# Edge-pair network on one core: a bias product moved from TensorE to GpSimd and VectorE for three of five chunks

## The chip, the cores and the metric

One core of a Trainium2 chip runs the whole program. The metric is the device time of one execution in microseconds. Runs that are compared are "fast" ones unless the text says otherwise; a run counts as slow when it takes over 1.5% longer than the fastest run of the same kernel. A ratio below is the mean time of one kernel's fast runs over the mean of the other kernel's fast runs of the same rounds, so it is not quite the ratio of the medians quoted beside it.

## The reference, cut to what matters

128 graphs of 64 nodes with 128 features. Every pair of nodes goes through a three-layer network with two layer norms, the result is weighted by the adjacency matrix and summed per node, and a second network of the same form updates the node.

```python
def _mlp(x, w0, b0, g0, be0, w1, b1, g1, be1, w2, b2):
    h = relu(x @ w0 + b0);  h = layernorm(h, g0, be0)
    h = relu(h @ w1 + b1);  h = layernorm(h, g1, be1)
    return h @ w2 + b2
messages = _mlp(concat(f_i, f_j), msg...) * adj[..., None]      # 64 x 64 pairs per graph
agg = sum(messages, axis=2)
updated = x + _mlp(concat(x, agg), upd...)
```

## The kernel before

Only real edges are computed, gathered into tiles of 128 edges: five tiles a graph, 20 for a "quartet" of four graphs, handled in chunks of four tiles, so five chunks a quartet. The first layer norm's scale is not applied to h. Instead the next bias is multiplied with each edge's standard deviation (std0), so that the scale can be taken out later: z = h·W1 + std0·b1. In the kernel before, TensorE makes std0·b1 too. The deviations are split into a high and a low part, transposed, and used as the stationary operand of one matmul of 512 columns in front of each chunk's layer-1 matmuls:

```python
def root_of(q):
    sd = root0(stp, V0[q], QT, "m20")                       # ScalarE: sqrt
    SH[q] = lp.tile([P, 4, QT], F32R, name="sh", bufs=2)
    sdb = sd.unsqueeze(1).to_broadcast([P, 2, QT])
    nc.scalar.copy(SH[q][:, 0:2, :], sdb)                   # high part
    nc.gpsimd.tensor_tensor(SH[q][:, 2:4, :], sdb, SH[q][:, 0:2, :].bitcast(F32),
                            op=ALU.subtract)                # low part
def turn_root(q):
    SD[q] = abank()
    nc.tensor.transpose(SD[q][0:4 * QT, 0:P], SH.pop(q)..., ident)
def layer1(n):
    q, c = divmod(n, QC)
    ps = ps_z.tile([P, CH, C], F32, name="z")               # one buffer
    nc.tensor.matmul(ps, lhsT=SD[q], rhs=W["b1t"][:, CH*c:CH*c+CH, :], start=True, stop=False, ...)
    for t in range(CH):
        nc.tensor.matmul(ps[:, t, :], lhsT=h[:, t*P:(t+1)*P], rhs=W["w1c"], start=False, ...)
    nc.scalar.activation(Y[n], ps, AF.Relu)                 # ScalarE empties z
```

Every instruction's place is fixed by hand in a plan of steps, one chunk a step; a block of eight graphs is ten steps. Each engine is given its instructions in that order, and the trace of the kernel before shows GpSimd's rows in it (`place` from 305.67 us, `marks_table` from 307.32, `odd_marks` from 308.62, the next w at 312.72):

```python
at(o - 8, "e", place, b); at(o - 8, "e", marks_table, b); at(o - 8, "e", odd_marks, b)   # GpSimd
at(n, "e1", var0_of, q); at(n + 1, "b", root_of, q)
at(n + 1, "x", turn_root, q); at(n + 2, "a", root_out, q)
# ... (updates, weights and reductions are placed in the same way)
for n in range(last + 1):
    run(n, "a"); run(n, "m")
    layer1(n - L1); run(n, "b"); layer0(n); stats0(n - 1); marks(n + 2); compare(n + 2); stats1(n - L1)
    for k in ("x", "x1", "x2", "e1", "e"): run(n, k)
```

## Time and profile before

| | before |
|---|---|
| median, range | 644.69 us, 641.02 to 645.77 (four runs, timed beside the change) |
| TensorE busy, mean granted clock | 96%, 0.993 |
| VectorE, ScalarE, GpSimd busy | 78%, 56%, 58% |
| one block of ten steps | 37.20 us, the same from step 36 on |

The block length is read from the timeline of TensorE: the distance from one start of a once-per-block operation to the next. It is the most useful number, since nearly the whole span repeats it.

The page's rows of 40 equal slices show busy tenths and, for PEclk, the granted clock in tenths:

```profile
PE   7899999999999999999999999999999999998875
PEclk8999999999999999999999999999999999999998
```

TensorE is busy 96% of the span at a mean granted clock of 0.993.

### The profile page before, as it was taken

Reading aid. Unit: us, or ns where it says so; the run is one execution under the profiler, and the core shown is the slowest. Engines: PE = TensorE matmul, PEld = TensorE weight load, DVE = VectorE, ACT = ScalarE, POOL = GpSimd, SP = SyncE. Lnnn points to the kernel's source line nnn. Section 1 sums busy time; section 2 is a strip of 40 time slices with the busy share of each in tenths; the row PEclk is TensorE's granted clock in tenths of the full one; section 3 lists DMA queues with packets and bytes.
Section 4 is the critical chain, followed back from the end, with each engine's and each line's share of the span. In section 5 each row is a group of like instructions: output and inputs, shape, how many; then the busy total and the mean of one; then the engine's idle time right before and its main releaser. Section 6 shows DMA issues by size and latency. Waiting matters only on the chain.

```text
span 639.0 us, 15850 instructions
## 1 busy us (share of the span) xinstructions
PE 615.1 (96%) x5875; PEld 567.0 (89%) x5875; DVE 497.6 (78%) x1894; ACT 358.6 (56%) x811; POOL 368.4 (58%) x943
## 2 busy tenths in 40 slices
PE   7899999999999999999999999999999999998875
PEld 6688899999999999999999999999999999997764
DVE  6787687878878787887878788787878877785574
ACT  3556556655656565565656556565655656563532
POOL 6742463847657384765738476573837657363653
PEclk8999999999999999999999999999999999999998
DMA  5100000010010101001010100101010000000001
GB/s 119 40 21 6 2 10 2 2 43 3 2 42 2 42 3 42 2 7 37 2 43 2 43 3 11 32 2 44 2 34 1 17 4 2 17 1 18 2 18 35
DMA packets 27916, 12.06 MB, mean 19 GB/s; under 512 B 10422, under 2 KB 27836, under 8 KB 27836
## 3 DMA queue, kind: packets, MB, share of 16 engines
q1 hardware_dynamic: 27548, 10.89, 6.4%
q8 instruction: 47, 0.77, 0.5%
q14 instruction: 33, 0.27, 0.1%
q10 hardware_dynamic: 288, 0.13, 0.1%
HBM read 6.82 MB, written 4.19 MB: 17 GB/s over the span
## 4 chain that ended last, share of the span: by engine, by line

## 5 line engine op out<-in xcount | busy, mean ns | idle before, releaser
L526 DVE BATCH_NORM_STATS2 st<-hT 128x6 f32<-128x128 f32 x640 | 141.1, 282 | 65.2 <-PE hT L522 62.6
L562 PEld LDWEIGHTS z<-w1c,h 128*128 128x128 f32 x1280 | 168.4, 192 | 7.1
L562 PE MATMUL z<-w1c,h 128*128 128x128 f32 x1280 | 168.8, 275 | 0.0
L641 POOL TENSOR_TENSOR w<-oh,m_q 128x320 f32<-128x320 f16 x124 | 86.9, 722 | 127.4 <-PE hT L522 110.9
L572 DVE BATCH_NORM_STATS2 st<-y 128x6 f32<-128x128 f32 x640 | 137.6, 276 | 6.0 <-ACT y L565 6.0
L565 ACT ACTIVATE y<-z 128x512 f32<-128x512 f32 x160 | 95.6, 597 | 81.4 <-PE z L562 79.5
L516 ACT ACTIVATE h<-hps,b0c 128x512 f32<-128x512 f32 x160 | 109.2, 682 | 6.1 <-PE hps L513 6.0
L505 DVE TENSOR_TENSOR s<-mk,cmpt 128x512 fp32r<-128x512 f32 x160 | 107.4, 672 | 0.4 <-PE mk L498 0.4
L522 PE MATMUL hT<-ident,h 128*128 128x128 f32 x640 | 97.0, 274 | 0.0
L513 PE MATMUL hps<-s,abl 128*128 128x512 f32 (+3 forms) x256 | 91.7, 370 | 0.0
L522 PEld LDWEIGHTS hT<-ident,h 128*128 128x128 f32 x640 | 76.2, 141 | 9.7
L559 PE MATMUL z<-b1t,sdT 80*128 80x512 f32 x160 | 78.8, 493 | 0.9 <-ACT y L565 0.9
L513 PE MATMUL hps<-s,abh 128*128 128x512 f32 (+3 forms) x256 | 78.1, 323 | 0.0
L656 PE MATMUL ys<-y,w 128*64 128x128 f32 x1280 | 76.9, 275 | 0.0
L656 PEld LDWEIGHTS ys<-y,w 128*64 128x64 f32 x1280 | 69.2, 137 | 3.4
L498 PE MATMUL mk<-tp,qs 128*128 128x512 f16 (+3 forms) x256 | 61.2, 300 | 1.8 <-DVE s L505 1.7
L473 DVE TENSOR_TENSOR abl<-mu,abh 128x512 fp32r<-128x512 f32 x32 | 22.1, 690 | 49.6 <-ACT abh L466 49.5
L632 ACT CAST oh<-ma 128x384 f16<-128x384 f32 (+1 forms) x128 | 48.6, 433 | 4.7 <-PE ma L625 1.8
L513 PEld LDWEIGHTS hps<-s,abl 128*128 128x128 f32 x256 | 49.2, 192 | 0.6 <-ACT h L516 0.3
L466 ACT CAST abh<-mu 128x512 fp32r<-128x512 f32 x32 | 18.7, 585 | 54.8 <-PE mu L459 54.8
L513 PEld LDWEIGHTS hps<-s,abh 128*128 128x128 f32 x256 | 49.1, 192 | 0.0
L559 PEld LDWEIGHTS z<-b1t,sdT 80*128 80x128 f32 x160 | 30.3, 190 | 8.9 <-issue 3.1
(235 smaller groups left out, 1036.8 us busy)
## 6 DMA issues: line engine op xcount, KB each, us to landing
xn<-in_x_dram SPq DMA_DIRECT2D x15, 256.0 KB, 3.2
out_dram<-uo SPq DMA_DIRECT2D x15, 256.0 KB, 2.2
an<-in_adj_dram SPq DMA_DIRECT2D x16, 128.0 KB, 2.9
xn<-in_x_dram SPq DMA_DIRECT2D x2, 128.0 KB
out_dram<-uo SPq DMA_DIRECT2D x2, 128.0 KB, 2.1
w<-in_L_gnn_msg_w_dram SPq DMA_DIRECT2D x2, 64.0 KB, 2.9
u<-in_L_gnn_upd_w_dram SPq DMA_DIRECT2D x2, 64.0 KB, 2.0
w0a<-in_L_gnn_msg_w_dram ACTq DMA_DIRECT2D x1, 64.0 KB, 2.1
```

What stands on the lines that cost most here:

```text
L498: nc.tensor.matmul(MK[n][:, c:c + w], lhsT=blocks[g // (2 * PB)]["qs"][:, g // 2 % PB, g % 2, :], rhs=TP[g // 2][:, e:e + w], start=True, ...
L505: nc.vector.tensor_tensor(S[n], MK.pop(n), cmpt[:, o:o + CH * P], op=ALU.is_equal)
L513: nc.tensor.matmul(ps[:, c:c + w], lhsT=ab[:, g % 4, :], rhs=s[:, c:c + w], start=(k == 0), stop=(k == 1))
L516: nc.scalar.activation(H[n], ps, AF.Relu, bias=b0c)
L522: nc.tensor.transpose(ps[:, t, :], H[n][:, t * P:(t + 1) * P], ident)
L526: nc.vector.bn_stats(ST0[q][:, CH * c + t, :], ps[:, t, :])
L559: nc.tensor.matmul(ps, lhsT=SD[q], rhs=W["b1t"][:, CH * c:CH * c + CH, :], start=True, stop=False, skip_group_check=True)
L562: nc.tensor.matmul(ps[:, t, :], lhsT=h[:, t * P:(t + 1) * P], rhs=W["w1c"], start=False, stop=True, skip_group_check=True)
L565: nc.scalar.activation(Y[n], ps, AF.Relu)
L572: nc.vector.bn_stats(ST1[q][:, CH * c + t, :], Y[n][:, t, :])
L641: (nc.vector if p // 2 == NQ - 1 else nc.gpsimd).tensor_tensor(w[:, :, g, :], OH[p][:, :, g, :], Q[q][:, k:k + TG].unsqueeze(2).to_broadca ...
L656: nc.tensor.matmul(YS[b][g * N:(g + 1) * N, k, :], lhsT=w[:, t, g, :], rhs=y, start=(t == 0), stop=(t == TG - 1))
```

## The change

The intent: TensorE is the bound, so take 96 of its 160 bias matmuls away. In chunks 0, 2 and 4, GpSimd computes the product std0·b1 and VectorE adds it to z and applies the relu, in place of ScalarE's eviction. To pay for that on VectorE, the odd-weight flag is counted on GpSimd, and the update's output is scaled on ScalarE and added to the residual on GpSimd.

```diff
-        def odd_weights(b):                        # VectorE
-            nc.vector.tensor_reduce(nball[:, b:b + 1], blocks[b].pop("a2")..., op=ALU.max, ...)
+        def even_marks(b):                         # GpSimd
             nc.gpsimd.tensor_tensor(a2, an, an, op=ALU.mult)
             nc.gpsimd.tensor_tensor(a2, a2, an, op=ALU.subtract)
+            nc.gpsimd.tensor_scalar(a2, a2, 0.0, None, op0=ALU.is_equal)
+            nc.gpsimd.tensor_tensor(even, even, a2, op=ALU.add)
+        PB1 = (1, 3)
+        KT = len(PB1) * CH
+        K1 = 4 * KT                                # 32 rows instead of 80
         def root_of(q):                            # splits only the 8 tiles of chunks 1 and 3
+            for k, c in enumerate(PB1):
+                nc.scalar.copy(SH[q][:, 0:2, s], sd)
+                nc.gpsimd.tensor_tensor(SH[q][:, 2:4, s], sd, SH[q][:, 0:2, s].bitcast(F32), ...)
+        def shift1(n):
+            SDB[n] = sbp.tile([P, CH, C], F32, name="sdb")
+            nc.gpsimd.tensor_tensor(SDB[n], bc(W["b1b"], CH), SD[q][...].to_broadcast(...), op=ALU.mult)
         def layer1(n):
-            nc.tensor.matmul(ps, lhsT=SD[q], ...)
+            if c in PB1:
+                nc.tensor.matmul(ps, lhsT=SDT[q], rhs=W["b1t"][:, k:k + CH, :], ...)
             for t in range(CH):
                 nc.tensor.matmul(ps[:, t, :], ..., start=c not in PB1, ...)
-            nc.scalar.activation(Y[n], ps, AF.Relu)
+            if c in PB1:
+                nc.scalar.activation(Y[n], ps, AF.Relu)
+            else:
+                add_relu(Y[n], ps, SDB.pop(n))     # VectorE
+        def scale_out(u):                          # ScalarE, then an add on GpSimd in finish
+            nc.scalar.activation(u.o[:, q, :], u.l_ps[:, q, :], AF.Copy, scale=u.q1[:, q:q + 1])
+            for c in range(QC):
+                if c not in PB1:
+                    at(n + 1 + c, "e1", shift1, q * QC + c)
# ... (table of the bias, the flag's last reduction and the tail's VectorE branch are cut)
```

## The prediction

> **What bounds the kernel now.** I read the page's busy shares first, then the groups by line, the waits, and the timelines of TensorE and GpSimd over one period.
>
> The first fence is from the page: busy time by engine, then four groups (line, engine, operation, out<-in, count | busy us, mean ns | idle before).
>
> ```profile
> PE 615.1 (96%) x5875; PEld 567.0 (89%) x5875; DVE 497.6 (78%) x1894; ACT 358.6 (56%) x811; POOL 368.4 (58%) x943
> ...
> L641 POOL TENSOR_TENSOR w<-oh,m_q 128x320 f32<-128x320 f16 x124 | 86.9, 722 | 127.4 <-PE hT L522 110.9
> ...
> L565 ACT ACTIVATE y<-z 128x512 f32<-128x512 f32 x160 | 95.6, 597 | 81.4 <-PE z L562 79.5
> ...
> L505 DVE TENSOR_TENSOR s<-mk,cmpt 128x512 fp32r<-128x512 f32 x160 | 107.4, 672 | 0.4 <-PE mk L498 0.4
> ...
> L559 PE MATMUL z<-b1t,sdT 80*128 80x512 f32 x160 | 78.8, 493 | 0.9 <-ACT y L565 0.9
> ```
>
> TensorE is busy 96% of the span and waits for almost nothing, so it sets the time. GpSimd at 58% looks free, with 127 us of idle time before its weights products (w). The question is where that idle time lies.
>
> The schedule is fixed in program order. One step handles a chunk of four edge tiles; five steps are a quartet of graphs, ten steps a block, and the pattern repeats with the block. I count steps 0 to 9 so that the two large "reduce" steps are 3 and 8. The timeline of TensorE (start, us, engine, line, operation):
>
> ```profile
> 284.51 0.48 PE L559 MATMUL z<-b1t,sdT 80*128 80x512 f32 x1
> 284.83 1.05 PE L562 MATMUL z<-w1c,h 128*128 128x128 f32 x8
> ...
> 293.10 0.48 PE L559 MATMUL z<-b1t,sdT 80*128 80x512 f32 x1
> ...
> 299.17 0.27 PE L546 MATMUL ma<-ident,sh 128*80 128x128 f32 x1
> ...
> 317.88 0.27 PE L546 MATMUL ma<-ident,sh 128*80 128x128 f32 x1
> ```
>
> Step 8 starts at 284.51, step 0 at 293.10. The next step 8 starts at 321.71 in the same view, so a block takes 37.20 us, and 16 blocks 595 of the 639 us. The L546 rows at the ends of steps 1 and 6 transpose the square roots (sh), whose low parts GpSimd writes; TensorE stands behind them in order. The timeline of GpSimd, same block:
>
> ```profile
> 295.42 1.40 POOL L641 TENSOR_TENSOR w<-oh,m_q 128x320 f32<-128x320 f16 x2 [6.98 <-PE hT L522]
> ...
> 298.74 0.27 POOL L541 TENSOR_TENSOR sh<-m_sd,sh 128x40 fp32r<-128x40 f32 x1 [0.68 <-ACT sh L540]
> ...
> 309.30 0.72 POOL L418 TENSOR_TENSOR a<-a,an 128x256 f32<-128x256 f32 x1
> ...
> 311.70 0.23 POOL L272 TENSOR_TENSOR m_v<-m_v,m 128x20 f32<-128x20 f32 x1
> 312.72 1.40 POOL L641 TENSOR_TENSOR w<-oh,m_q 128x320 f32<-128x320 f16 x2 [0.80 <-DVE m_q L283]
> ...
> 316.30 0.27 POOL L541 TENSOR_TENSOR sh<-m_sd,sh 128x40 fp32r<-128x40 f32 x1 [0.68 <-ACT sh L540]
> ```
>
> This carries the prediction. GpSimd's idle time is one hole of 6.98 us in front of step 0's weights. From there to step 5's weights it works through 17 us with only 0.68 and 0.80 us idle: residual and bias of the update, placement, marks table, odd marks, variance. Its second sh ends at 316.57, only 1.31 us before TensorE's transpose at 317.88; in step 1 it ends at 299.01, 0.16 us before. The wait list agrees that this is every block: step 0's w waits 110.9 us in 17 times, step 5's 16.5 us in 14 (1.2 us each).
>
> [...] a 128x512 add takes GpSimd 1284 ns (xo), a two-input VectorE compare of that size 672. [...] The trace has 0.32 us from the bias matmul to the next (284.51 to 284.83), [...] I use 0.32. GpSimd's rows come in program order. [...]
>
> **The change part by part.**
> - TensorE: three of five bias matmuls go, six a block: 6 x 0.32 = 1.92 us of 37.20. Over 16 blocks 31 us, were nothing else to wait.
> - ScalarE: 96 evictions of 597 ns go. The update's output is scaled there instead, about 1.1 us a block (four times about 0.27 us, the 265 ns of a 128x128 PSUM copy). It has room.
> - VectorE: 96 add-and-relu of 128x512 come in, 0.67 us each as the existing uy one (64 us); 16 reduces of 0.40 us and 60 scalings of 0.34 us go (27 us). About 535 us, still under the span.
> - GpSimd, per block: six products of bias and std0 of 128x512, each 1.04 us as the same product in the update (usdb, 1039 ns); two further sh operations, 0.27 each; two more operations for the even count, an add of 0.73 and a comparison with a constant of 128x256, which has no row (about 0.8, my estimate from 260 ns at 20 columns and 618 at 128 with a per-partition scalar); an add of 1.28 in the output. In all 9.6 us on top of 23 us, so about 33 of 37. That fits on average, but not where it falls.
>
> The order of GpSimd's instructions in the changed kernel puts one product in step 0, ahead of the variance, one in step 1, one in step 3, and the even count in step 2: all inside the full stretch. One more is in step 5 before that variance. So:
> - Now from the w at 295.42 to the end of the second sh at 316.57: 21.15 us.
> - Added: 4 products 4.16, two sh 0.54, even count 1.55; the idle 0.80 is filled. 21.15 + 6.25 - 0.80 = 26.60 us.
> - TensorE wants that sh now 22.46 us after the w (317.88 - 295.42). It will wait until 26.60.
> - From that transpose to the next block's w is 37.20 - 22.46 = 14.74 us, set by TensorE and VectorE; two bias matmuls less (steps 7, 8) make 14.10.
> - New block: 26.60 + 14.10 = **40.70 us**, against 37.20: +3.5 us.
> Part of the wait shows in step 1: sh is 1.04 + 0.27 later, TensorE 0.32 earlier, slack 0.16, hence some 1.4 us idle there; the rest in steps 5 and 6. The product for step 5 comes after the same backlog, so VectorE's add waits for it, and with it the only z buffer. This overlaps the sh wait and isn't added.
>
> The full stretch needs both updates (from step 23) and placement (to about step 142): 12 blocks, +42 us. The four lighter ones keep little of the TensorE saving because step 1's wait stays; I take -2. Sum: +40 us, **684 us**.
>
> **The rivals.**
> - TensorE stays the bound: -31 us, 613. For it: 96% busy, and GpSimd's mean load under 90%. Against: the 0.16 and 1.31 us of slack before the two transposes. It needs the backlog to vanish.
> - VectorE becomes the bound: z has one buffer, and in three of five steps its release moves to VectorE, behind the update's layers. VectorE's 535 us lie under the span and TensorE's reduce steps of 6 us let it catch up; alone it would hold the time near 620 to 640. It would waste the gain, not lengthen the span much.
> - The clock: waits of 2 to 3 us in each block may drop TensorE's granted clock, now 0.993. [...]
>
> **Range and chances.** If the comparison costs 0.5 us more or less, the total moves 6 us; if a further 0.8 us of overlap is found per block, 10 us[...]. So 662 to 704. I leave 12% for a GpSimd stretch that starts earlier than I think: 0.05 faster, 0.07 within 2%.
>
> **What would show it.** Right: GpSimd runs without a gap from step 0 to step 5's weights, its hole before step 0 shrinks to about 4 us; TensorE waits for sh (L541's successor) or for VectorE's add, itself waiting for sdb, some 5 us a block; TensorE falls below 90% busy; a block takes 40 to 41 us. Wrong: sdb products well under 1 us, sh ready before TensorE arrives, TensorE still at 95%, blocks under 37 us. If blocks are near 37 us with VectorE waits naming z, the second rival holds.

The cut passages told of the hardware from elsewhere, or put a size on the fallen clock that no trace had given. The sum has lost no term: +42 - 2 = +40 us, 684 us. The range 662 to 704 has: beside the two terms that still stand (6 and 10 us) it held an estimate for the clock. That waits of 2 to 3 us can drop the clock was the author's guess then; the changed kernel's trace shows it (half clock at a wait of 2.95 us, below).

## The result, and the profile after

The changed kernel takes 742.19 us (741.97 to 743.59, four runs) against 644.69 us for the kernel before. The ratio of the fast runs is 1.153, 95% interval 1.148 to 1.158. The outputs agree with the reference. The direction was predicted; the size was not: +97.5 us where +40 was forecast.

A block now takes 44.37 us (44.37 to 44.42 from step 56 on). In the views below, sdb is GpSimd's product, z the PSUM buffer of layer 1 and y its output after the relu, sh the split roots, and w the weights product with which a block begins on GpSimd; CUSTOM_DVE_ANT_0 (in e2_noprod also _1) is the profile's name for what the kernel's `add_relu` issues at L247. First the page after: the busy line, the slices, and five groups.

```profile
PE 657.5 (89%) x5779; PEld 581.2 (78%) x5779; DVE 549.4 (74%) x1912; ACT 324.9 (44%) x809; POOL 509.7 (69%) x1116
...
PE   7799899898989989899898989989899898999774
...
PEclk9899999999998989989898998989989898999977
...
L653 POOL TENSOR_TENSOR w<-oh,m_q 128x320 f32<-128x320 f16 x124 | 87.0, 723 | 82.7 <-PE mk L495 75.9
...
L563 POOL TENSOR_TENSOR sdb<-b1b,m_sd 128x512 f32<-128x512 f32 x96 | 99.9, 1041 | 0.0
...
L247 DVE CUSTOM_DVE_ANT_0 y<-z,sdb 128x512 f32<-128x512 f32 x96 | 64.8, 675 | 14.5 <-PE z L578 4.9
...
L575 PE MATMUL z<-b1t,sdT 32*128 32x512 f32 x64 | 34.5, 540 | 38.9 <-DVE y L247 37.9
...
L581 ACT ACTIVATE y<-z 128x512 f32<-128x512 f32 x64 | 38.3, 598 | 67.7 <-PE z L578 67.7
```

No engine is above 89%. GpSimd's product costs 1041 ns as read off its sibling before (usdb, 1039 ns), and VectorE's add 675 ns. The new thing is the fourth group: TensorE stands idle for 38 us in front of bias matmuls until VectorE has emptied z. And the clock row has lost its even nines: the mean granted clock is 0.932.

Step 6 on TensorE in the kernel before (start, us, engine, line, operation):

```profile
313.17 0.48 PE L559 MATMUL z<-b1t,sdT 80*128 80x512 f32 x1
313.48 1.05 PE L562 MATMUL z<-w1c,h 128*128 128x128 f32 x8
```

One block on TensorE after, steps 5 to 9 (the same columns, then idle before and releaser):

```profile
309.28 0.60 PE L713 MATMUL ma<-ident,ysum 128*128 128x128 f32 x4
312.83 0.79 PE L575 MATMUL z<-b1t,sdT 32*128 32x512 f32 x1 [2.95 <-DVE y L247]
313.55 2.08 PE L578 MATMUL z<-w1c,h 128*128 128x128 f32 x8
...
320.64 0.27 PE L551 MATMUL ma<-ident,sh 128*32 128x128 f32 x1
...
330.00 0.49 PE L575 MATMUL z<-b1t,sdT 32*128 32x512 f32 x1
330.42 1.16 PE L578 MATMUL z<-w1c,h 128*128 128x128 f32 x8
```

In front of step 6 TensorE waits 2.95 us for VectorE's add. Then the same eight matmuls that took 1.05 us before take 2.08. The transpose of sh at 320.64 shows no wait at all.

VectorE's add of step 5, and GpSimd's timeline of the same block:

```profile
312.09 0.69 DVE L247 CUSTOM_DVE_ANT_0 y<-z,sdb 128x512 f32<-128x512 f32 x1 [0.38 <-POOL sdb L563]
```

```profile
290.70 1.40 POOL L653 TENSOR_TENSOR w<-oh,m_q 128x320 f32<-128x320 f16 x2 [5.09 <-PE mk L495]
...
310.83 0.23 POOL L272 TENSOR_TENSOR m_v<-m_v,m 128x20 f32<-128x20 f32 x1
311.01 1.04 POOL L563 TENSOR_TENSOR sdb<-b1b,m_sd 128x512 f32<-128x512 f32 x1
312.01 1.41 POOL L653 TENSOR_TENSOR w<-oh,m_q 128x320 f32<-128x320 f16 x2
...
316.77 0.36 POOL L546 TENSOR_TENSOR sh<-m_sd,sh 128x8 fp32r<-128x8 f32 x2 [0.86 <-ACT sh L545]
...
335.10 1.40 POOL L653 TENSOR_TENSOR w<-oh,m_q 128x320 f32<-128x320 f16 x2 [5.11 <-PE mk L495]
```

GpSimd works from the w at 290.70 to the one at 312.01, just behind the sdb that step 5 needs, with one idle time of 0.65 us (at 295.14, for ScalarE's part of sh), and then has a hole of 5.1 us in front of the next block. The sdb ends at 312.05, VectorE starts at 312.09, TensorE at 312.83. That is the whole chain of the wait.

The view of windows shows the clock of this block. The columns after the stretch are its length, then busy us of TensorE, its weight loads, VectorE, ScalarE and GpSimd, then the granted clock, the DMA share and GB/s.

```profile
305.00:310.00 5.00, 4.88 (x42) 4.28 (x41) 2.65 (x10) 2.26 (x6) 4.57 (x11) 1.00 0.00 0
310.00:315.00 5.00, 2.17 (x8) 1.73 (x8) 3.19 (x12) 1.85 (x4) 4.75 (x11) 0.72 0.00 0
315.00:317.50 2.50, 2.50 (x12) 2.34 (x12) 0.82 (x2) 1.72 (x5) 1.47 (x5) 0.50 0.00 0
317.50:320.00 2.50, 2.50 (x18) 2.34 (x16) 2.26 (x9) 0.00 (x0) 1.99 (x3) 0.70 0.00 0
320.00:325.00 5.00, 5.00 (x45) 4.82 (x44) 4.44 (x16) 2.38 (x8) 1.20 (x6) 1.00 0.02 3
```

TensorE was granted half its clock from about 312.2 to 319.0, 6.8 us. It got it back after the wait was long over. In the same place of ten blocks in the trace there is a stretch of 6.8 us at half clock, and in the two blocks before these one of 3.4 us.

The trace's record of the granted clock shows something more. It lists each drop with its start and length. In the changed kernel's trace there are 17, and the later 16 start a whole multiple of 3.413 us after the first (to 0.01 us), so the drops of this trace lie on a grid, and 44.37 us is 13 times 3.413. (The trace before has two drops, 182 times 3.413 us apart.) The blocks settled at 44.37 us (they took 43.1 us while the drop lasted 3.4 us). That the grid holds them there is my reading; no run tests it.

So the block as measured: 21.35 us from the w to the end of step 5's sdb, 0.78 through VectorE to TensorE's start, 7.81 for step 6 (312.83 to 320.64; it was 4.71 before, 313.17 to 317.88), 14.46 to the next w. The sum is 44.40.

### The profile page after: what moved, and what is told of

Same layout as the page of the kernel before. It is cut to its first block, busy times and chain, and to the rows that moved or that the text cites. A ratio compares the mean times of both kernels' runs of the same rounds, so it can differ in the third digit from the quotient of the medians.

```text
span 740.4 us, 15865 instructions
## 1 busy us (share of the span) xinstructions
PE 657.5 (89%) x5779; PEld 581.2 (78%) x5779; DVE 549.4 (74%) x1912; ACT 324.9 (44%) x809; POOL 509.7 (69%) x1116
## 4 chain that ended last, share of the span: by engine, by line
## 5 line engine op out<-in xcount | busy, mean ns | idle before, releaser
L578 PE MATMUL z<-w1c,h 128*128 128x128 f32 x1280 | 191.3, 295 | 5.4 <-DVE y L247 5.2
L519 PE MATMUL hT<-ident,h 128*128 128x128 f32 x640 | 102.3, 285 | 0.0
L563 POOL TENSOR_TENSOR sdb<-b1b,m_sd 128x512 f32<-128x512 f32 x96 | 99.9, 1041 | 0.0
L510 PE MATMUL hps<-s,abl 128*128 128x512 f32 (+3 forms) x256 | 96.5, 386 | 0.0
L519 PEld LDWEIGHTS hT<-ident,h 128*128 128x128 f32 x640 | 80.6, 147 | 10.3 <-DVE st L523 0.2
L510 PE MATMUL hps<-s,abh 128*128 128x512 f32 (+3 forms) x256 | 81.7, 337 | 0.0
L247 DVE CUSTOM_DVE_ANT_0 y<-z,sdb 128x512 f32<-128x512 f32 x96 | 64.8, 675 | 14.5 <-PE z L578 4.9
L575 PE MATMUL z<-b1t,sdT 32*128 32x512 f32 x64 | 34.5, 540 | 38.9 <-DVE y L247 37.9
L581 ACT ACTIVATE y<-z 128x512 f32<-128x512 f32 x64 | 38.3, 598 | 67.7 <-PE z L578 67.7
L575 PEld LDWEIGHTS z<-b1t,sdT 32*128 32x128 f32 x64 | 12.6, 197 | 51.9 <-DVE y L247 46.0
```

The lines of the kernel that those rows point to most:

```text
L247: nc.vector._custom_dve(TENSOR_ADD_SAT, out=o, in0=ps, in1=sb, s0=BIG, s1=0.0)
L510: nc.tensor.matmul(ps[:, c:c + w], lhsT=ab[:, g % 4, :], rhs=s[:, c:c + w], start=(k == 0), stop=(k == 1))
L519: nc.tensor.transpose(ps[:, t, :], H[n][:, t * P:(t + 1) * P], ident)
L563: nc.gpsimd.tensor_tensor(SDB[n], bc(W["b1b"], CH), SD[q][:, CH * c:CH * c + CH].unsqueeze(2).to_broadcast([P, CH, C]), op=ALU.mult)
L578: nc.tensor.matmul(ps[:, t, :], lhsT=h[:, t * P:(t + 1) * P], rhs=W["w1c"], start=c not in PB1, stop=True, skip_group_check=True)
```

## The experiments

Theory A: the program order of GpSimd's queue puts more work between step 0 and step 5 than fits; its late product makes VectorE's add late, and with it the only z buffer; the idle time so made drops TensorE's clock, which costs a second time. Rival B: VectorE's added 0.67 us in three of five steps is the bound in itself. All kernels below gave correct results except where said. The diffs are shortened to the lines that matter. "Before" was timed beside each group (medians 643.1 to 645.2 us).

| kernel | median us | ratio to before (95%) | block us | clock in the profile |
|---|---|---|---|---|
| the change | 742.19 | 1.153 (1.148 to 1.158) | 44.37 | 0.932 |
| e1_fill | 709.27 | 1.102 (1.098 to 1.107) | 41.49 | 0.991 |
| e2_noprod (wrong on purpose) | 673.32 | 1.045 (1.040 to 1.050) | 38.91 | 0.982 |
| e3_noeven | 683.28 | 1.062 (1.057 to 1.066) | 39.71 | 0.988 |
| e4_late | 738.53 | 1.143 (1.135 to 1.151) | 42.2 to 45.1 | 0.953 |
| e5_move | 673.65 | 1.048 (1.042 to 1.054) | 38.82 | 0.986 |
| e6_movelate | 684.42 | 1.063 (1.058 to 1.069) | 39.18 | 0.976 |
| e7_prods (on before) | 677.10 | 1.053 (1.047 to 1.059) | 39.55 | 0.988 |
| e8_noscale | 738.13 | 1.147 (1.142 to 1.152) | 44.37 | 0.939 |
| e9_before_move (on before) | 646.00 | 1.003 (0.998 to 1.009) | 37.20 | 0.986 |
| e10_k80 | 676.96 | 1.052 (1.047 to 1.058) | 38.4, or 40.0 where the clock falls | 0.967 |
| e11_best | 650.96 | 1.013 (1.008 to 1.017) | 36.88 | 0.986 |
| e12_best_nv | 640.32 | 0.995 (0.990 to 0.999) | 36.85 | 0.984 |

### e1_fill: keep TensorE busy in the gap

```diff
+        def keep_busy():
+            warm2 = ubank()
+            for k in range(10):
+                nc.tensor.matmul(warm2[:, 0:P], lhsT=mean_m, rhs=mean_m, start=True, stop=True)
+        for b in range(2, NB - 1):
+            at(b * CPB + 5, "x2", keep_busy)
```

> The changed kernel with ten idle 128x128 matmuls (about 2.1 us) put into step 5 of each block, in the gap where TensorE waits for VectorE's add. Theory A (GpSimd's queue makes a gap of 3 us; in the gap TensorE's granted clock falls to half for 6.8 us, which costs another 3.4 us a block): clock back to 0.98 or more, blocks fall from 44.4 to about 41 us (26.4 of GpSimd's stretch plus 14.5), time 698 to 712 us. Rival B (VectorE, with the added add-and-relu, sets the block and the low clock is only a sign of an idle TensorE): clock goes up, time stays within 1% of 742.

Adding work made it 33 us faster: 709.27 us. From the views of the cores, the changed kernel and this one:

```profile
core 0: 740.4 us, clock 0.932
```

```profile
core 0: 703.7 us, clock 0.991
```

The idle matmuls took 2.40 us a block. Blocks fell from 44.37 to 41.49 us; the views from 340 to 385 us show the clock at 1.00 throughout, and in the full blocks no group of matmuls is slow any more. The first slow one comes at 681.72 us, in the tail of the 704 (ys, 3.86 us, against 2.40 at 331.12). B's forecast (time unchanged) is refuted. The clock is a cost of its own, 2.9 us a block.

### e2_noprod: VectorE's work kept, GpSimd's products gone

```diff
-                add_relu(Y[n], ps, SDB.pop(n))
+                add_relu(Y[n], ps, bc(W["b1b"], CH))
-            for c in range(QC):
-                if c not in PB1:
-                    at(n + 1 + c, "e1", shift1, q * QC + c)
```

> The changed kernel with VectorE's add-and-relu kept as it is, but reading the bias itself instead of the product, so GpSimd makes no products (wrong result on purpose). Theory A: GpSimd's stretch loses 4.2 us (26.4 to 22.2), no long gap, clock near 0.99, blocks 36 to 37.5 us, time 625 to 655 us. Rival B (VectorE sets the block): VectorE does the same work, so time stays above 700 us.

673.32 us: 69 of the 97 us go with GpSimd's products, though VectorE does just what it did; the fallen clock's share is in that (0.982 now). But it is 18 us above A's range. The timelines of VectorE and TensorE in step 2 and 3 show a part of what is left:

```profile
312.63 0.68 DVE L247 CUSTOM_DVE_ANT_0 uy<-mu,usdb 128x512 f32<-128x512 f32 x1
313.34 0.87 DVE L737 BATCH_NORM_STATS2 uy_st<-uy 128x6 f32<-128x128 f32 x4
314.13 0.67 DVE L247 CUSTOM_DVE_ANT_1 y<-z,b1b 128x512 f32<-128x512 f32 x1
```

```profile
314.86 1.16 PE L578 MATMUL z<-w1c,h 128*128 128x128 f32 x8 [1.22 <-DVE y L247]
```

In step 2 VectorE runs the update's layer first and the add after it, so TensorE waits 1.22 us for z. B has a share: about 1.2 us a block here. A part of the rest is the subject of e10.

### e3_noeven: the flag back on VectorE

```diff
-            nc.gpsimd.tensor_scalar(a2, a2, 0.0, None, op0=ALU.is_equal)
-            nc.gpsimd.tensor_tensor(even, even, a2, op=ALU.add)
+            blocks[b]["a2"] = a2            # and the reduce on VectorE as before
```

> The changed kernel with the odd-weight flag back as before (reduce on VectorE, no comparison and add on GpSimd). Theory A: GpSimd's stretch loses 1.74 us; the gap shrinks from 3.1 to about 1.4 us, so blocks fall to 42.6 if the clock still drops and to 39 or less if it doesn't: time 660 to 722 us. Rival B: VectorE gets 0.32 us a block more, time the same or up to 1% longer.

683.28 us. Taking 1.74 us of GpSimd's work out of each block gained 4.66 us a block, since the clock no longer falls at the shorter gap (no group of matmuls is slow in the full blocks; mean clock 0.988 against 0.932). The last wait of the block is plain in TensorE's timeline:

```profile
355.74 0.29 PE L555 MATMUL ma<-ident,sh 128*32 128x128 f32 x1 [0.62 <-POOL sh L550]
...
371.21 0.50 PE L579 MATMUL z<-b1t,sdT 32*128 32x512 f32 x1 [1.12 <-DVE y L247]
```

The gap in front of step 6 is 1.12 us instead of 2.95. Against e1 (clock up, even count still there) the block is 1.78 us shorter: the even count's own 1.74.

### e4_late: TensorE no longer waits for sh

```diff
-            at(n + 1, "x", turn_root, q)
+            at(n + 2, "x", turn_root, q)
-            at(n + 2, "a", root_out, q)
+            at(n + 3, "a", root_out, q)
```

> The changed kernel with the transpose of the roots (and its copy) one step later; the first chunk that uses it comes two steps later, so TensorE never waits for sh. If the wait for sh were what holds the block (the step as predicted), blocks lose about 3.5 us or more and the time falls below 700 us. If the product for step 5, VectorE's add behind it and the single z buffer hold it just as long (what the trace after shows), only the small wait of step 1 goes: time within 2% of 742, 728 to 745 us.

738.53 us, 0.5% less than the change. So the wait for sh, on which the prediction built its sum, is not what holds the block. (TensorE doesn't wait for GpSimd's sh here, but the later transpose waits 0.65 us a block for ScalarE, as in e6_movelate below.) This run's TensorE still waits for VectorE's add behind the late product:

```profile
443.90 0.49 PE L575 MATMUL z<-b1t,sdT 32*128 32x512 f32 x1 [2.93 <-DVE y L247]
```

### e5_move: GpSimd's work moved into its hole

```diff
-                at(o - 8, "e", place, b)
-                at(o - 8, "e", marks_table, b)
-                at(o - 8, "e", even_marks, b)
+                at(o - 8 if b < 2 else o - 11, "e", place, b)
+                at(o - 8 if b < 2 else o - 11, "e", marks_table, b)
+                at(o - 8 if b < 2 else o - 11, "e", even_marks, b)
```

> The changed kernel with placement, marks table and even count (6.2 us of GpSimd's work) moved from step 2 to step 9 of the block before, where GpSimd has its hole. Theory A: the stretch from step 0 to step 5 loses the 6.2 us; the hole is 5.1 us, so step 0 starts 1 us late; no wait for step 5's product, clock near 0.99; left are step 1's wait for sh (1.5 to 2.5 us) and VectorE's 1.2 us in step 3. Blocks 37.5 to 39 us, time 645 to 675 us. Rival B: no work leaves VectorE or TensorE, time above 700.

673.65 us, inside the range, with the same amount of work on every engine as in the change: only its place in GpSimd's order moved. Left in TensorE's timeline is the wait of step 1:

```profile
390.88 0.28 PE L551 MATMUL ma<-ident,sh 128*32 128x128 f32 x1 [1.49 <-POOL sh L546]
```

### e6_movelate: both

This joins the edits of e4_late and e5_move.

> The move of the run before and the later transpose together. If step 1's wait for sh is what the move leaves, blocks fall by another 1.5 to 2 us to 36 to 37 us and the time to 625 to 645 us; if VectorE's add in front of the single z buffer is what is left, they stay within 0.5 us of the move alone.

684.42 us, 1.6% slower than the move alone, where 625 to 645 or no change was expected: the time is a miss. The blocks (39.18 against 38.82) lie within the 0.5 us of the second branch. The later transpose no longer waits for GpSimd, but now takes its place in the rotation of the two PSUM buffers "ma" behind ScalarE:

```profile
380.64 0.27 PE L551 MATMUL ma<-ident,sh 128*32 128x128 f32 x1 [0.65 <-ACT cumall L376]
```

At the start of step 3 TensorE also waits 0.82 us for VectorE's add. The wait of 1.49 us was traded for two others. The move is the better place to work.

### e7_prods: GpSimd's load alone, on the kernel before

```diff
+            for c in (0, 2, 4):
+                at(n + 1 + c, "e1", shift1, q * QC + c)      # product made, never read
```

> The kernel before, with the three products of bias and std0 per quartet computed on GpSimd at the same places as in the changed kernel, but not used: TensorE, VectorE and ScalarE do what they did. Theory A: GpSimd's stretch grows from 21.15 by 4.16 less 0.80 to 24.5 us, and with the 14.74 us of the rest a block takes 39.2 us instead of 37.2; time 660 to 680 us, clock still near 0.99. Rival B (GpSimd's load is harmless, VectorE's added work is what costs): 640 to 650 us as before.

677.10 us and blocks of 39.55, against 39.2 worked out ahead. Nothing was added to VectorE or TensorE here. The predicted wait appears, in steps 1 and 6:

```profile
313.64 0.31 PE L547 MATMUL ma<-ident,sh 128*80 128x128 f32 x1 [0.81 <-POOL sh L542]
...
333.69 0.31 PE L547 MATMUL ma<-ident,sh 128*80 128x128 f32 x1 [0.34 <-POOL sh L542]
```

A third wait, 0.53 us in front of step 6's z (328.45), is for ScalarE's eviction of z. ScalarE had stood 2.18 us for GpSimd's late variance (m_v, at 327.61), so it comes from the same queue.

### e8_noscale: the output's scaling back on VectorE

```diff
-                at(n + t[14], "b", scale_out, u)
-                at(n + t[14], "e", finish, u)
+                at(n + t[14], "m", finish, u)          # VectorE, as before
```

> The changed kernel with only the output's scaling put back on VectorE. GpSimd's add of 1.28 us goes from the leg that has the hole, and VectorE gets its 1.03 us in step 8, where it waits 2 us for the rows. Theory A: nothing on the path moves, time within 1% of 742 us. If this part carried a share of the loss, the time falls by its share, 1.28 us a block or 20 us.

738.13 us and the same 44.37 us a block. This part of the change lies beside the path of the full blocks. Since 44.37 us is also the length at which blocks settle on the clock's grid, the earlier blocks are the better witness, and they agree too: with a drop of 3.4 us they take 43.1 us in both kernels.

### e9_before_move: the move as a control

The edit of e5_move, on the kernel before (with odd_marks).

> The kernel before with placement, marks table and odd marks moved from step 2 to step 9 in the same way, as a control. TensorE bounds that kernel and waits for nothing there, so the time stays within 0.7% of before (640 to 650 us). If it falls by more, GpSimd's queue cost the kernel before something too, and the gain of the move isn't one of the change.

646.00 us, ratio 1.003 with 1 inside the interval, blocks 37.20. GpSimd's order cost the kernel before nothing, so what the move gains in the changed kernel is a debt of the change.

### e10_k80: the bias operand with 80 rows again

```diff
-        K1 = 4 * KT
+        K1 = 4 * QT                       # 80 rows; the table holds chunks 1 and 3 alone
+            SH[q] = lp.tile([P, 4, QT], F32R, name="sh", bufs=2)   # one copy and one subtraction
```

The move of e5_move is in it too.

> The move of GpSimd's 6.2 us again, and the roots split for all 20 tiles as in the kernel before, so that the bias matmul's stationary operand has 80 rows instead of 32 (zeros in the table for the rest), with one sh operation instead of two. If the 32-row operand is why the steps that keep the bias matmul now take 0.2 us longer (2.81 against 2.60 us) and eat TensorE's saving, these steps go back to 2.60 to 2.65 us; with sh 0.3 us earlier in step 1 blocks fall from 38.8 to 37.5 to 38.0 us and the time to 650 to 662 us. If the rows don't matter, steps 4 and 9 stay at 2.8 us and blocks at 38.5.

The time missed its range (676.96 us), the mechanism did not. Step 9, from the bias matmul to the next step's start, takes 2.62 us (419.71 to 422.33) against 2.81 in the changed kernel (330.00 to 332.81) and 2.60 before:

```profile
419.71 0.50 PE L573 MATMUL z<-b1t,sdT 80*128 80x512 f32 x1
420.04 1.05 PE L576 MATMUL z<-w1c,h 128*128 128x128 f32 x8
...
422.33 1.11 PE L576 MATMUL z<-w1c,h 128*128 128x128 f32 x8
...
430.69 0.31 PE L549 MATMUL ma<-ident,sh 128*80 128x128 f32 x1 [2.04 <-POOL sh L544]
```

From the bias matmul to the next one is 0.33 us again, where the 32-row one takes 0.42, and the group after it is back from 1.16 to 1.05 us. Four steps a block keep the matmul. Against e5_move, steps 4, 6 and 9 got 0.2 us shorter each (2.82 to 2.63, 5.03 to 4.82, 2.82 to 2.62); in step 1 the wait for sh hides it. What was won so was lost in the last line: TensorE reaches sh earlier and waits 2.04 us, and after five of eleven such waits the matmuls run at about half speed for some 3.4 us (from 236.9 to 240.3, say, where four hT take 1.06 us, against 0.60 at 198.60), which makes those blocks 40.0 us long instead of 38.4.

### e11_best and e12_best_nv: the causes taken away together

```diff
-        PB1 = (1, 3)
+        PB1 = (3, 4)                      # VectorE adds in chunks 0, 1, 2
+        K1 = 4 * QT                       # 80 rows
+                at(o - 8 if b < 2 else o - 11, "e", place, b)        # marks_table stays at o - 8
+                at(o - 8 if b < 2 else o - 11, "e", even_marks, b)
```

e12_best_nv also puts the flag and the output's scaling back on VectorE, as in the kernel before.

> All causes taken away at once: 80 rows; placement and even count moved to step 9 (marks table left in step 2, so that step 0 isn't late); and the bias matmul kept for chunks 3 and 4 rather than 1 and 3, so that GpSimd's products no longer stand ahead of the variance and VectorE's add no longer stands behind the update's layers in steps 2 and 7. If waiting for GpSimd, VectorE's queue in front of the single z buffer and the 32 rows are the whole loss, TensorE's six matmuls a block (1.9 us) show at last: blocks 35.5 to 36.7 us, time 615 to 635 us, 1 to 4% faster than before. If blocks stay at 37 or more, another cost is left that I have not named.

> The run before without the two smaller parts of the change: flag counted on VectorE and output scaled on VectorE, as in the kernel before. They give VectorE back 1.4 us a block and take 3 us from GpSimd. Where TensorE bounds, both kernels agree within 1%; if VectorE bounds, this one is 1 to 3% slower; if GpSimd still bounds, 1 to 3% faster.

Both reach blocks of 36.9 us, the first ones shorter than 37.20. That is above what I expected (35.5 to 36.7), and e11's time missed its range (615 to 635 us) too. e12_best_nv takes 640.32 us, ratio 0.995 (0.990 to 0.999): the only kernel here with a time below that of the kernel before, by half a per cent, so within the 2% that counts as the same. e11_best is 1.3% slower than before (650 to 651 us in its three fast timed runs; one more, at 652.62, counted as slow), while its profiled run took 642.92. By the times, its two extra parts cost 1.6%, the size of my third branch; in the profiled runs they cost nothing in a block (36.88 against 36.85) and 1.2 us in all. No trace of a run of 650 us was kept, so where that time goes, and why its runs differ, stays open.

The lengths of the ten steps, each from the start of its first layer-1 matmul to the next step's, say where the predicted 1.92 us went. "Bias" marks the steps that keep the bias matmul in e12:

| step | 0 | 1 | 2 | 3 | 4 | 5 | 6 | 7 | 8 | 9 | sum |
|---|---|---|---|---|---|---|---|---|---|---|---|
| before, us | 2.68 | 3.42 | 2.15 | 6.09 | 2.61 | 3.12 | 4.73 | 3.81 | 5.99 | 2.60 | 37.20 |
| e12, us | 2.74 | 3.44 | 2.34 | 5.67 | 3.05 | 2.90 | 4.75 | 3.81 | 5.76 | 2.39 | 36.85 |
| e12 | | bias | bias | | | | bias | bias | | | |

Where nothing waits (steps 5, 8 and 9) a removed matmul saves 0.22, 0.23 and 0.21 us, not 0.32. Steps 2 and 3 together save 0.23 (without its bias matmul step 3 counts as starting later). In steps 0 and 4 the saving is eaten by VectorE: the next z waits for its add, in the profile 0.07 us at the end of step 0 and 0.40 us at that of step 4:

```profile
418.36 1.16 PE L580 MATMUL z<-w1c,h 128*128 128x128 f32 x8 [0.40 <-DVE y L247]
```

## Why the prediction was right or wrong

- **What bounds before, and that mean load is not the question: right.** GpSimd's stretch between step 0 and step 6's sh measured 26.4 us (290.70 to 317.13); 26.60 was worked out. Its hole shrank to 5.1 us; "about 4" was said. e7_prods and e9_before_move show both halves of the argument on the kernel before.
- **Added costs: right.** Product 1041 ns (1.04 predicted), VectorE's add 675 (0.67), even count 0.87 + 0.73 (0.8 + 0.73), TensorE 89% busy ("below 90%"). The scaling on ScalarE took 384 ns, not about 270, beside the path. VectorE was busy for 549 us, not 535. An old instruction got slower: the 128x640 f16 comparison (tp) rose from a mean of 383 to 590 ns (up to 1401), 13 us in all. In the changed kernel's block from 289 us one of its four rows takes 1.40 us (at 300.22) and the others 0.35 to 0.37; in e2_noprod's from 292 us, without GpSimd's products, all four take 0.35 to 0.37. What slowed it was not shown, nor that it was on the path.
- **"TensorE wants that sh ... It will wait until 26.60": wrong as to the wait.** At 320.64 TensorE doesn't wait for sh, and e4_late, which removes the wait, gains 0.5%. The binding wait is the one that the prediction named in passing and didn't add up: step 5's product, VectorE's add, the one z buffer (no run tried a second one). It happens to be nearly as long, which is why the block without the clock's part, 41.49 us in e1_fill, came out near 40.70. That agreement is luck. The wait of step 1, "some 1.4 us", measured 0.64.
- **The clock: the step that failed.** The third rival said that waits of 2 to 3 us "may drop TensorE's granted clock", with the clock then at 0.993; the size it gave that was an estimate that no trace had shown. The fallen clock took 33 us (742.19 against 709.27 in e1_fill), the largest missing term. The prediction had worked out a wait of that length in every block, and then gave its consequence a side place instead of a term in the block's sum. That term measured 2.9 us a block (44.37 against 41.49), so over the 12 full blocks 32 us.
- **"6 x 0.32 = 1.92 us" of TensorE's saving: mis-sized.** The start-to-start interval of 0.32 us doesn't go whole: in the traces, the matmul behind a bias matmul takes 0.11 us to its next one (before), and the first of a chunk without one 0.11 to 0.21 (after). 0.22 us is what a removed matmul gives back where nothing waits (steps 5, 8 and 9). The 32-row operand then costs the remaining ones 0.2 us each (e10_k80; seen in three of four). By my estimate from these figures that is 1.3 us won and 0.8 lost a block for TensorE, so half a microsecond in place of 1.92.
- **"The four lighter ones ... I take -2": wrong.** Up to step 26 the changed kernel had lost 6.4 us (a 6.8-us stretch at half clock at 28.9 us is in it), and in the last steps, after step 146, it lost 11.2. There the low clock returns several times: the last 40 us have a mean clock of 0.77 against 0.93 before. How much of the tail is the clock and how much the queues was not tested apart.
- **VectorE as a rival: partly right.** It doesn't set the block, but 1.2 us a block in e2_noprod, and 0.4 us in one step of e12, are its.

Together: between steps 26 and 146, the 12 full blocks, the loss is 83.8 us (529.27 against 445.49); +42 was predicted for them. With the clock up (e1_fill) they lose 51.5 (496.95), so of the 42 us that the prediction missed there 32 are the clock's and 10 the sum's.

## What to carry to other kernels

An engine's mean load says little where its order is fixed: find its holes, and add the new work to the stretch between two of them, up to the instruction that someone else waits for. When that sum shows TensorE idle in each period for as long as the clock fell for here (2.95 us in every block, 2.9 in nine blocks of twelve in e4_late, 2.04 in five of eleven in e10_k80, 1.5 in none), put the fallen clock into the sum too (2.9 us a block here); filling such a gap with idle matmuls can pay (742.19 to 709.27 us, e1_fill), and moving the work pays more (673.65 us, e5_move). And take what a removed matmul gives back where nothing waits (0.22 us here), not its start-to-start interval (0.32), as the value of removing it.

## What the runs show of the clock and of the 32-row operand

- The clock, in the changed kernel's trace, fell 2.3 us into an idle gap of 2.95 us (309.88 to 312.83, half clock from about 312.2), and at that gap in every full block (in the first two it fell 0.4 and 1.7 us behind the gap's end, in the other ten 2.2 to 2.5 us into it). In e10_k80 the matmuls slowed after five of eleven gaps of 2.02 to 2.05 us, in e4_late after nine of twelve gaps of 2.90 to 2.93. Behind the gaps of 1.1 and 1.5 us in the full blocks of e3_noeven and e5_move none slowed. What parts the gaps with a drop from those without was not shown. In the clock records of the kernel before and of the changed one, every low stretch is at one half and 3.41 or 6.83 us long, save the last one, which runs to the end of the kernel (7.94 and 6.96 us).
- The 32-row operand: the weight load in front of the bias matmul takes about the same (median 182 ns with 32 rows, 190 ns with 80 rows in the kernel before), but a 32-row operand cost more in what follows it: 0.42 us to the next matmul and a following group of 1.16 us, against 0.33 and 1.05 with 80 rows (e10_k80). Why was not shown.
